# Layer 0's attention scores by column groups, with block transposes on VectorE and first sums as small products, in a two-layer attention kernel

## The chip, the cores and the metric

The kernel runs on one core of one Trainium2 chip. The core has five engines that work side by side, each with its own stream of instructions, which it runs in order, and which meet through semaphores: PE (TensorE, matrix products into PSUM), DVE (VectorE), ACT (ScalarE), POOL (GpSimd) and SP (which here only issues DMAs). The metric is device time in microseconds of one execution; lower is better.

## The reference, cut to what matters

The input `x` is 8 batches of 64 x 16 = 1024 tokens with 128 channels. Layer 0 is attention with 8 heads and a feed-forward part, with two softmaxes in a row over the keys, first over the 64 rows `m` and then over the 16 columns `g` of the 64 x 16 grid:

```python
q = proj(wq, bq); k = proj(wk, bk); v = proj(wv, bv)
scores = jnp.einsum('bhlfc,bhmgc->bhlfmg', q, k) / jnp.sqrt(jnp.float32(c))
a = jax.nn.softmax(scores, axis=4)
a = jax.nn.softmax(a, axis=5)
z = jnp.einsum('bhlfmg,bhmgc->bhlfc', a, v)
...
return _layer_norm(ffy + z1, ln2_g, ln2_b)
```

Layer 1 has an additive attention and a recurrence. For all pairs of the 1024 tokens of a batch it needs

```python
scores = jnp.einsum('d,bijd->bij', v, jnp.tanh(Wi[:, None, :, :] + Wi[:, :, None, :]))
```

and the recurrence `yt = sigmoid(wx_t + yt @ Vt)` runs over the tokens at the end.

## The kernel before

**An order written out by a planner.** `layer0` and `layer1` issue nothing themselves. They call `add`, which notes a piece of work: its engine (or a choice of engines) with an estimated cost, what it reads and writes, and a priority. `Plan.emit` (line 529) then simulates the engines with these costs and the latencies of lines 499 and 500 and writes every engine's instructions out in the order it finds. The order is fixed when the kernel is built; on the chip an engine that has to wait holds up all that stands behind it. `Bank` picks a free PSUM bank at that time, and `through_bank` (line 843) is the usual pair of a product into a bank and its eviction. For PE the planner knows two modes, "full" and "groups" (products of 32 array columns, four of which work side by side), and counts 0.1 us for a change.

**Layer 0** (line 872) goes over 8 heads and, in a head, 8 query tiles of 128 queries, 512 tiles over all batches. Keys and queries are folded into one matrix `A`, values and output into `Wvo`; `u` (line 903) is the projected query side and `vp` (line 917) the values. One tile does:

- scores (line 939, PE): two products of 512 columns into `sc`, 128 queries on the partitions and 1024 keys along them;
- the exponential (line 942, ACT), in place in PSUM;
- first sums over `m` (line 946, DVE), 1024 elements to 16, their inverse (949) and the division (952, DVE) from PSUM into `e` in SBUF. `sc` has two buffers and is free after that;
- for a pair of tiles: second exponential (963, ACT, 2048 elements), second sums over `g` (966, DVE), inverse (969), and the second division (980, POOL), in place;
- eight transposes of 128 x 128 (line 853, PE) a tile, four into a bank, each bank copied to `aT` (line 865, DVE, or 863, ACT, in batch 0), so that keys lie on partitions;
- attending (line 994, PE): for a pair of tiles eight products of 256 columns with `vp`, and their addition to `zs` (1001, DVE).

`e` has two buffers of a pair (`NE`), `aT` two. After the heads come a layer norm, the feed-forward part (lines 1041 to 1065, whose hidden values lie in an `aT`) and a second norm.

**Layer 1** (line 1218) takes the upper half of the token pairs in groups of rows. A row is `wiT` plus one column of it. Either ACT adds and takes the tanh at once (line 1107), or POOL or DVE (1117, 1111) add several rows into the ring `th` and ACT takes one wide tanh over them (line 1165). PE multiplies them with the vector `v` in column groups (line 1185) into `sa`. Which engine adds a row is the planner's choice, by which is free first and by the `fillers` of lines 1253 to 1261.

**Order.** Batch 0's layer 0 starts alone (`alone`), in two halves; it keeps the values of all eight heads in the ring `th`, and uses four banks in the first half. From then on layer 0 of batch b + 1 runs beside layer 1 of batch b. The last batch's layer 1 is alone again, and the recurrence (lines 1478 to 1520) ends the kernel.

Of the kernel before, what the change touches and what calls it, by code (L numbers as in the profile page):

```python
# [11 lines left out]
ALU = mybir.AluOpType  # L12
# [621 lines left out]
def fast_path(ctx: ExitStack, tc: tile.TileContext, a: dict, fits):  # L634
# [16 lines left out]
    NE = 2  # L651
# [11 lines left out]
    def ring(name, n, shape, pool=work):  # L663
        return [tile_of(pool, f"{name}{i}", shape) for i in range(n)]
# [20 lines left out]
    room = 20 * N  # L685
# [4 lines left out]
    aTs = ring("aT", 2, [P, NT, 2 * P])  # L690
    es = [wx[:, 4 + 2 * i : 6 + 2 * i, :] for i in range(NE)]
# [51 lines left out]


# [92 lines left out]
    count = {"aT": 0}  # L837

    def next_aT():
        count["aT"] += 1  # L840
        return (count["aT"] - 1) % 2

    def through_bank(pe, weight, r, evict, where, more, w, pri, choice=two):

        bank = Bank(*choice)
        n = len(plan.ops)
        add(("PE", weight), lambda _: pe(bank()), r=r, w=[("bank", n)], pri=pri, take=bank, wait=more + w)
        add(where, lambda e: evict(e, bank()), r=[("bank", n)] + more, w=w, pri=pri, give=bank)
# [23 lines left out]
    def layer0(b):  # L872
        alone = b == 0
        STRETCH = 0.95 if b < NB - 1 else 1.25
        xT, kx = xTs[b % 2], ("xT", b % 2)
        kz = ("zs",)
# [12 lines left out]
        for n_part, part in enumerate(parts):  # L889
# [3 lines left out]
            for h in range(H):  # L893
# [3 lines left out]
                if alone:  # L897
                    vp, kvp = th[:, (12 + h) * N : (13 + h) * N].rearrange("p (t c) -> p t c", c=C), ("vp0", h)
                for s in range(2) if part is None else (part,):
                    cols = slice(s * 512, (s + 1) * 512)  # L900

                    def project(bank, h=h, cols=cols):
                        nc.tensor.matmul(bank, A[:, h, :], xT[:, cols], start=True, stop=True)  # L903
# [20 lines left out]
                for qt in qts:  # L924
# [3 lines left out]
                    pair, q = (b * H * NT + i) // 2 % NE, qt % 2  # L928
# [3 lines left out]
                    r1, r2 = st[:, q, 0:G], st[:, :, G : G + M]  # L932
                    sc3 = sc.rearrange("p (m g) -> p m g", g=G)
                    e3 = e.rearrange("p (m g) -> p m g", g=G)

                    def scores(_, sc=sc, u=u, qt=qt):
                        for s in range(2):
                            cols = slice(s * 512, (s + 1) * 512)
                            nc.tensor.matmul(sc[:, cols], u[:, qt * P : (qt + 1) * P], xT[:, cols], start=True, stop=True)  # L939

                    add(("PE", 1.74), scores, r=[kx, ("u", h % 2, qt // 4)], w=[kc], pri=L0)
                    add(("ACT", 0.98), lambda _, sc=sc: nc.scalar.activation(sc, sc, AF.Exp, scale=SCALE),  # L942
                        r=[kc], w=[kc], pri=L0)

                    def first_sums(_, sc=sc, r1=r1):
                        nc.vector.tensor_reduce(r1, sc.rearrange("p (m g) -> p g m", g=G), AX.X, ALU.add)  # L946

                    def first_inverse(_, r1=r1):
                        nc.vector.reciprocal(r1, r1)

                    def divide(_, e3=e3, sc3=sc3, r1=r1):
                        nc.vector.tensor_tensor(e3, sc3, r1.unsqueeze(1).to_broadcast([P, M, G]), ALU.mult)  # L952

                    add(("DVE", 1.15), first_sums, r=[kc], w=[k1], pri=L0)
                    add(("DVE", 0.2), first_inverse, r=[k1], w=[k1], pri=L0)
                    add(("DVE", 1.22), divide, r=[kc, k1], w=[ke], pri=L0)
# [16 lines left out]
                    na = next_aT()  # L973
                    aT = aTs[na]
                    for q in range(2):
# [7 lines left out]
                        for s in range(2):  # L983
                            through_bank(
                                transposes([e[:, t * P : (t + 1) * P] for t in range(4 * s, 4 * s + 4)]), 0.52, [ke],
                                copy(aT[:, 4 * s : 4 * s + 4, q * P : (q + 1) * P]), evict(0.68), [],
                                [("aT", na, q, s)], L0, banks,
                            )
# [3 lines left out]
                    def attend(part, vp=vp, aT=aT, bank=bank):  # L992
                        for t in range(4 * part, 4 * part + 4):
                            nc.tensor.matmul(bank()[:, :256], vp[:, t, :], aT[:, t, :], start=t == 0, stop=t == NT - 1)  # L994

                    def gather(_, h=h, q0=q0, bank=bank):
                        zq = zs[:, q0 : q0 + 2 * P]
                        if h == 0:
                            nc.vector.scalar_tensor_tensor(zq, bank()[:, :256], zb, xT[:, q0 : q0 + 2 * P], ALU.add, ALU.add)
# [3 lines left out]
                    for s in range(2):  # L1003
                        add(
                            ("PE", 1.74), lambda _, attend=attend, s=s: attend(s),
                            r=[kvp + (p,) for p in range(2)] + [("aT", na, q, p) for q in range(2) for p in range(2)],
# [5 lines left out]
            for qh in range(2) if part is None else (part,):  # L1012
# [22 lines left out]
                na = next_aT()  # L1035
                hT = aTs[na].rearrange("p t q -> p (t q)").rearrange("p (f q) -> p f q", q=512)
                kh = [("aT", na, q, s) for q in range(2) for s in range(2)]
                for f in range(NFF):
# [10 lines left out]
                    through_bank(hidden, 0.9, [k1], relu, evict(0.75), kh[:1] if f else [], kh if f == 0 else [kh[f]], L0, banks)  # L1049
# [35 lines left out]
    def group(it, at0, r0, k, wiT, all_wi, L1, ROWS, fillers, chain, left, both, first_half):  # L1085
# [11 lines left out]
        slot = Span(ring_room, at[4], 12 * N if first_half else 20 * N)  # L1097
# [257 lines left out]
    def fetch_wx():  # L1355
        keys = [[("u", i, s) for s in range(2)] for i in range(2)]
        keys += [[("vp", i, s) for s in range(2)] for i in range(2)] + [[("e", i, q), ("e", i, 2)] for i in range(NE) for q in range(2)]
# [230 lines left out]
```

## Time and profile before

| | |
|---|---|
| median of 3 runs | 5320.47 us (5319.22 to 5320.98) |
| the profiled execution | 5316.93 us |
| its span, first to last instruction | 5315.0 us |
| granted clock of TensorE | 0.993 |
| share of the chain that ended last: scores, transposes, attending | 13%, 8%, 13% |
| share of the same chain: tanh times v | 25% |
| tanh on ACT: wide (997), single rows (1904) | 2734.8 us, 1369.8 us busy |

In the profile a group of instructions is given by its line, engine, operation, what it writes and reads, its shape and its count; then come the us in which it was busy, the mean ns of one, and the idle time of the engine before it with what ended that idle time. PE is the stream of products and PEld that of weight loads, which overlaps it. Ends of products are modelled, so PE's busy share is not its share at full speed.

### The profile page before, as it was taken

What the parts mean: (1) busy time and instruction counts of PE and PEld (TensorE: products, weight loads), DVE (VectorE), ACT (ScalarE), POOL (GpSimd) and SP (SyncE); (2) the same over time, 40 slices, a digit from 0 to 9 for tenths busy, and PEclk for the clock granted to TensorE, in tenths of its full rate; (3) what the DMA queues carried; (4) which work ended last, traced back from release to release, by engine and by line L of the source; (5) the groups of instructions that cost most, each with busy time, mean ns of one, the idle gap of its engine ahead of it and who ended that gap; (6) DMA issues with size and microseconds to landing.
All of it is one profiled execution on the core that took longest, in us unless ns stands there. A gap on an engine that the chain in (4) does not pass through costs nothing.

```text
span 5315.0 us, 98773 instructions
## 1 busy us (share of the span) xinstructions
PE 5007.1 (94%) x39173; PEld 2763.8 (52%) x39173; DVE 4884.6 (92%) x8676; ACT 5057.1 (95%) x4042; POOL 4522.8 (85%) x3113
## 2 busy tenths in 40 slices
PE   8899999999999999999999999999999999986567
PEld 6555555555555555555555455555555455542125
DVE  7899999999999999999999999999999999988885
ACT  5489999999999999999999999999999999999994
POOL 2365779899998999999998999999899999987991
PEclk9999999999999999999999999999999999999999
DMA  2000000000000000000000000000000000000001
GB/s 62 1 5 1 1 1 5 1 9 1 1 5 7 3 1 5 5 5 1 1 5 5 5 1 1 5 6 4 1 1 3 7 1 1 1 29 9 1 1 69
DMA packets 27335, 37.68 MB, mean 7 GB/s; under 512 B 2512, under 2 KB 19280, under 8 KB 26864
## 3 DMA queue, kind: packets, MB, share of 16 engines
q1 hardware_dynamic: 24832, 27.99, 1.6%
q8 instruction: 310, 5.08, 0.4%
q10 hardware_dynamic: 1872, 3.16, 0.2%
q14 instruction: 161, 1.32, 0.1%
q0 software_dynamic: 160, 0.13, 0.0%
HBM read 19.22 MB, written 12.06 MB: 6 GB/s over the span
## 4 chain that ended last, share of the span: by engine, by line
PE 67%; ACT 16%; DVE 10%; issue 6%; POOL 1%; DMA 0%; ACTq 0%; DVEq 0%; SPq 0%; POOLq 0%
PE sa L1185 25%; PE m L994 13%; PE sc L939 13%; ACT th L1165 9%; PE m L853 8%; ACT th L1107 4%; DVE th L1111 2%; PE m L1314 2%; PE m L917 2%; DVE stat_e L966 2%; PE m L903 1%; DVE stat_e L946 1%; ACT wx L963 1%; ACT sc L942 1%; DVE aT L865 1%
## 5 line engine op out<-in xcount | busy, mean ns | idle before, releaser
L1117 POOL TENSOR_TENSOR th<-wiT 128x1024 f32<-128x1024 f32 (+59 forms) x2303 | 3345.5, 1487 | 215.2 <-PE sa L1185 196.0
L1165 ACT ACTIVATE th<-th 128x2634 f32<-128x2634 f32 (+53 forms) x997 | 2734.8, 2774 | 9.3 <-DVE th L1117 6.0
L1185 PE MATMUL sa<-th,vpat 128*32 128x512 f32 (+36 forms) x24576 | 2009.0, 459 | 202.2 <-ACT th L1165 186.9
L1111 DVE TENSOR_SCALAR_CACHE_REDUCE th<-wiT 128x344 f32<-128x344 f32 (+59 forms) x1930 | 1602.9, 867 | 68.6 <-PE sa L1185 65.8
L1107 ACT ACTIVATE th<-wiT 128x512 f32<-128x512 f32 (+62 forms) x1904 | 1369.8, 793 | 11.8 <-PE sa L1185 11.8
L1185 PEld LDWEIGHTS sa<-th,vpat 128*32 128x32 f32 x24576 | 652.2, 110 | 1319.1 <-issue 842.2
L980 POOL TENSOR_TENSOR wx<-wx,stat_e 128x1024 f32<-128x1024 f32 x512 | 981.6, 1938 | 398.9 <-DVE stat_e L969 213.7
L939 PE MATMUL sc<-xT,wx 128*128 128x512 f32 x2048 | 983.5, 605 | 13.1 <-DVE wx L952 11.9
L994 PE MATMUL m<-aT,wx 128*128 128x256 f32 x3584 | 824.6, 384 | 7.2 <-DVE aT L865 7.2
L994 PEld LDWEIGHTS m<-aT,wx 128*128 128x128 f32 x3584 | 673.5, 191 | 187.8 <-issue 51.9
L865 DVE COPY aT<-m 128x512 f32<-128x512 f32 x940 | 616.6, 684 | 67.6 <-PE m L853 64.3
L946 DVE TENSOR_REDUCE stat_e<-sc 128x16 f32<-128x1024 f32 x512 | 613.5, 1204 | 38.9 <-ACT sc L942 37.7
L966 DVE TENSOR_REDUCE stat_e<-wx 128x128 f32<-128x2048 f32 x256 | 583.6, 2280 | 52.5 <-ACT wx L963 51.9
L952 DVE TENSOR_TENSOR wx<-sc,stat_e 128x1024 f32<-128x1024 f32 x512 | 619.9, 1214 | 3.2
L853 PEld LDWEIGHTS m<-ident,wx 128*128 128x128 f32 x3968 | 445.2, 141 | 309.4 <-issue 168.8
L942 ACT ACTIVATE sc<-sc 128x1024 f32<-128x1024 f32 x512 | 515.2, 1010 | 69.0 <-PE sc L939 52.8
L853 PE MATMUL m<-ident,wx 128*128 128x128 f32 x3968 | 558.6, 278 | 12.5 <-DVE aT L865 6.9
L939 PEld LDWEIGHTS sc<-xT,wx 128*128 128x128 f32 x2048 | 355.4, 191 | 385.8 <-issue 334.3
L963 ACT ACTIVATE wx<-wx 128x2048 f32<-128x2048 f32 x256 | 487.6, 1905 | 15.7 <-DVE wx L952 15.6
L969 DVE RECIPROCAL stat_e<-stat_e 128x128 f32<-128x128 f32 x256 | 240.9, 941 | 0.1
L1111 DVE DVE_READ_ACCUMULATOR th<-wiT 128x1 f32 x1930 | 160.8, 83 | 0.0
L917 PEld LDWEIGHTS m<-Wvo,xT 128*128 128x128 f32 x1080 | 133.9, 193 | 51.2 <-issue 25.0
(182 smaller groups left out, 2835.5 us busy)
## 6 DMA issues: line engine op xcount, KB each, us to landing
xT<-in_xt_dram SPq DMA_DIRECT2D x8, 512.0 KB, 3.6
th<-in_x_dram SPq DMA_DIRECT2D x8, 512.0 KB, 6.8
parked<-X SPq DMA_DIRECT2D x16, 256.0 KB, 2.3
xr<-parked SPq DMA_DIRECT2D x8, 512.0 KB, 8.1
parked_wx<-bT SPq DMA_DIRECT2D x14, 256.0 KB, 2.0
wx<-parked_wx SPq DMA_DIRECT2D x7, 512.0 KB, 3.2
out_dram<-ot ACTq DMA_DIRECT2D x8, 256.0 KB, 3.2
out_dram<-ot SPq DMA_DIRECT2D x8, 256.0 KB, 3.2
```

The costliest lines, as they stand in the source:

```text
L853: nc.tensor.transpose(bank[:, i * P : (i + 1) * P], s, ident)
L865: nc.vector.tensor_copy(dst, src)
L939: nc.tensor.matmul(sc[:, cols], u[:, qt * P : (qt + 1) * P], xT[:, cols], start=True, stop=True)
L946: nc.vector.tensor_reduce(r1, sc.rearrange("p (m g) -> p g m", g=G), AX.X, ALU.add)
L966: nc.vector.tensor_reduce(r2, e2.rearrange("p q (m g) -> p q m g", g=G), AX.X, ALU.add)
L980: nc.gpsimd.tensor_tensor(e3, e3, r2[:, q, :].unsqueeze(2).to_broadcast([P, M, G]), ALU.mult)
L994: nc.tensor.matmul(bank()[:, :256], vp[:, t, :], aT[:, t, :], start=t == 0, stop=t == NT - 1)
L1107: nc.scalar.activation(rows(c)[:, r, :], wiT[:, i0 + begin[c] :], AF.Tanh, bias=w_i(c, r))
L1111: nc.vector.tensor_scalar(rows(c)[:, r, :], wiT[:, i0 + begin[c] :], w_i(c, r), 0.0, ALU.add, ALU.add, accum_out=next_unused())
L1117: eng.tensor_tensor(rows(c), wiT[:, i0 + begin[c] :].unsqueeze(1).to_broadcast(shape), w_i(c).unsqueeze(2).to_broadcast(shape), ALU.add,)
L1165: nc.scalar.activation(slot()[:, a:z], slot()[:, a:z], AF.Tanh)
L1185: nc.tensor.matmul(sa[32 * c : 32 * c + 32, s:s1], vpat[:, 31 - r0 - r : 63 - r0 - r], rows(c)[:, r, s - at0 - begin[c] : s1 - at0 - begin ...
```

## The change

**Token order.** `xT` is now laid out by the host so that keys can be taken by quarters: token 256 a + 32 b + r stands at place 128 b + 32 a + r. `tokens` is a view of it by quarter `a`.

**Scores.** For each 32 queries (`s`) and each quarter of the keys (`a`) there is one product of 32 array columns and 256 keys, 16 a tile, in PE's "groups" mode. On partition 32 a + r lies query r of every block `s`, with the 256 keys of quarter `a`, for four values of `s` one after the other.

**First softmax.** The exponential goes from `sc` straight to `e`. Since a query's keys are now on four partitions, the first sums are products: 16 of 64 columns with `same_row` (a one where the partitions' numbers agree modulo 32) add over quarters and over four of the columns' parts, and a reduction of 64 elements on DVE finishes them. After the inverse, 16 products of 16 columns with slices of `ident` spread the result back to the four partitions, and DVE's division reads it from PSUM. The other branch (`by_pe` false) is not built.

**Transposes.** After the second division DVE transposes `e` in place in blocks of 32 x 32. With the keys' order this puts keys on partitions, so PE's transposes, their copies and `aT` are gone, and attending reads `e` itself, in runs of 32.

**Room.** `e` has three buffers, and the feed-forward part keeps its hidden values in one of them. The ring grows by 448 elements a partition; batch 0's values of heads 6 and 7 lie in `X1` and `B1`.

```diff
-    NE = 2
+    NE = 3
...
-    aTs = ring("aT", 2, [P, NT, 2 * P])
-    es = [wx[:, 4 + 2 * i : 6 + 2 * i, :] for i in range(NE)]
+    es = [wx[:, 4 + 2 * i : 6 + 2 * i, :] for i in range(2)] + ring("e", NE - 2, [P, 2, N])
...
+    same_row = tile_of(const, "same_row", [P, 32])
+    nc.vector.tensor_reduce(same_row, ident.rearrange("p (a r) -> p r a", a=4), AX.X, ALU.add)
...
+        tokens = xT.rearrange("p (b a r) -> p a b r", a=4, r=32)
...
                     def scores(_, sc=sc, u=u, qt=qt):
-                        for s in range(2):
-                            cols = slice(s * 512, (s + 1) * 512)
-                            nc.tensor.matmul(sc[:, cols], u[:, qt * P : (qt + 1) * P], xT[:, cols], start=True, stop=True)
+                        for s in range(4):
+                            rows = slice(qt * P + 32 * s, qt * P + 32 * s + 32)
+                            for a in range(4):
+                                nc.tensor.matmul(
+                                    sc[32 * a : 32 * a + 32, 256 * s : 256 * s + 256], u[:, rows],
+                                    tokens[:, a], start=True, stop=True,
+                                )
...
-                    add(("DVE", 1.15), first_sums, r=[kc], w=[k1], pri=L0)
-                    add(("DVE", 0.2), first_inverse, r=[k1], w=[k1], pri=L0)
-                    add(("DVE", 1.22), divide, r=[kc, k1], w=[ke], pri=L0)
...
+                        def sums(bank, e=e):
+                            for i in range(4):
+                                for s in range(4):
+                                    cols = slice(256 * s + 64 * i, 256 * s + 64 * i + 64)
+                                    nc.tensor.matmul(
+                                        bank[32 * s : 32 * s + 32, 0:64], same_row, e[:, cols], start=i == 0, stop=i == 3
+                                    )
...
+                        def last_sums(_, bank, s1=s1):
+                            nc.vector.tensor_reduce(
+                                s1, bank[:, 0:64].rearrange("p (m g) -> p g m", g=G), AX.X, ALU.add
+                            )
...
+                        through_bank(sums, 0.45, [ke], last_sums, ("DVE", 0.2), [], [k1], L0, banks, "groups")
...
+                        def spread(bank, r1=r1):
+                            for s in range(4):
+                                for a in range(4):
+                                    nc.tensor.matmul(
+                                        bank[32 * a : 32 * a + 32, s * G : s * G + G], ident[:, 32 * s : 32 * s + 32], r1,
+                                        start=True, stop=True,
+                                    )
...
+                        add(("DVE", 0.2), first_inverse, r=[k1], w=[k1], pri=L0)
+                        through_bank(spread, 0.3, [k1], divide, ("DVE", 1.22), [ke], [ke], L0, banks, "groups")
...
-                        for s in range(2):
-                            through_bank(
-                                transposes([e[:, t * P : (t + 1) * P] for t in range(4 * s, 4 * s + 4)]), 0.52, [ke],
-                                copy(aT[:, 4 * s : 4 * s + 4, q * P : (q + 1) * P]), evict(0.68), [],
-                                [("aT", na, q, s)], L0, banks,
-                            )
+                        add(("DVE", 1.17), lambda _, e=e: nc.vector.transpose(e, e), r=[ke], w=[ke], pri=L0)
...
+                    keys = e2.rearrange("p q (s b r) -> p b (q s) r", s=4, r=32)
...
-        "xt": np.asarray(x).reshape(NB, N, C).transpose(0, 2, 1),
+        "xt": np.asarray(x).reshape(NB, 4, 8, 32, C).transpose(0, 4, 2, 1, 3).reshape(NB, C, N),
```

## The prediction

> **What bounds the kernel now.** I read the page's busy shares and chain first, then busy time by stage, then the groups, then single stretches of TensorE's timeline.
>
> ```profile
> PE 5007.1 (94%) x39173; PEld 2763.8 (52%) x39173; DVE 4884.6 (92%) x8676; ACT 5057.1 (95%) x4042; POOL 4522.8 (85%) x3113
> ...
> PE 67%; ACT 16%; DVE 10%; issue 6%; POOL 1%; DMA 0%; ACTq 0%; DVEq 0%; SPq 0%; POOLq 0%
> ```
> ```profile
> 0.00:315.00 315.00, 282.19 (x1299) 197.81 (x1300) 259.80 (x359) 168.94 (x297) 113.07 (x76) 0.99 0.10 27
> 315.00:890.00 575.00, 565.42 (x3929) 324.01 (x3928) 539.51 (x806) 556.81 (x625) 419.72 (x263) 1.00 0.01 3
> 890.00:4490.00 3600.00, 3542.85 (x28053) 1936.49 (x28051) 3392.83 (x5937) 3573.75 (x2583) 3350.18 (x2306) 1.00 0.01 4
> ...
> 4800.00:5105.00 305.00, 181.03 (x2039) 59.28 (x2043) 259.77 (x531) 305.00 (x144) 253.37 (x166) 0.96 0.01 4
> ```
>
> A line of the second view gives, for a stretch, the busy us of PE, PEld, DVE, ACT, POOL, then the clock, the DMA share and GB/s. From 890 to 4490 us, six batches of about 600 us, ACT is busy 99%, PE 98%, DVE 94% and POOL 93%: nothing has room, and no one edit moves the end unless the others give way too. PE's ends are modelled, so 98% overstates it. From start to start its work for one batch is: 64 query tiles x 1.72 (scores) = 110; 64 x 0.87 (transposes) = 56; 32 x 3.45 (attending) = 110; 4.22 million tanh columns / 8 batches / 4 groups x 1.67 ns = 220, and 4 ns for each of 768 rounds, 3; projections, values, layer 1's products and FFN about 58; sum 557. The built order changes between full products and column groups 1730 times, 216 a batch at about 0.09 us: 19. So 576 of 600, 96%. ACT, whose durations are real, is the tighter bound; PE follows within 3%. In the first 315 us batch 0's layer 0 runs alone and DVE (218 of the 240 us from 60 to 300) leads; from 4800 ACT is never idle.
>
> ```profile
> L1165 ACT ACTIVATE th<-th 128x2634 f32<-128x2634 f32 (+53 forms) x997 | 2734.8, 2774 | 9.3 <-DVE th L1117 6.0
> ...
> L1107 ACT ACTIVATE th<-wiT 128x512 f32<-128x512 f32 (+62 forms) x1904 | 1369.8, 793 | 11.8 <-PE sa L1185 11.8
> ...
> L865 DVE COPY aT<-m 128x512 f32<-128x512 f32 x940 | 616.6, 684 | 67.6 <-PE m L853 64.3
> L946 DVE TENSOR_REDUCE stat_e<-sc 128x16 f32<-128x1024 f32 x512 | 613.5, 1204 | 38.9 <-ACT sc L942 37.7
> L966 DVE TENSOR_REDUCE stat_e<-wx 128x128 f32<-128x2048 f32 x256 | 583.6, 2280 | 52.5 <-ACT wx L963 51.9
> L952 DVE TENSOR_TENSOR wx<-sc,stat_e 128x1024 f32<-128x1024 f32 x512 | 619.9, 1214 | 3.2
> ```
> ```profile
> 276.95 1.88 PE L939 MATMUL sc<-xT,wx 128*128 128x512 f32 x4
> 278.67 1.04 PE L853 MATMUL m<-ident,wx 128*128 128x128 f32 x8
> 279.54 1.88 PE L939 MATMUL sc<-xT,wx 128*128 128x512 f32 x4
> ...
> 4361.02 1.09 PE L1185 MATMUL sa<-th,vpat 128*32 128x64 f32 x64
> 4362.04 1.98 PE L939 MATMUL sc<-xT,wx 128*128 128x512 f32 x4
> ```
>
> In the timeline the difference of two starts is what a piece costs: scores 1.72 us, eight transposes 0.87. The second stretch is the row nearest to the new small products: 64 records in column groups (each f32 product makes two), 61 to 64 columns wide, in 1.02 us with the change of mode behind them, four running side by side.
>
> **The change, part by part, for one query tile (512 in all).**
>
> *Scores.* Two products of 512 columns become 16 of 256 on 32 array columns, four at a time. L1185 shows that form: a round of four records takes its columns over 1.2 per ns and about 4 ns. Eight rounds of 256 columns: 8 x 0.218 = 1.74 us against 1.72. Equal. The operand is now read in runs of 32; no row here has that at this size. I take nothing; the far end is a tenth, 0.17 us.
>
> *Transposes go from PE (-0.87).* In their place PE gets sums, eight rounds of 64 columns, 8 x 0.058 = 0.46, and the spreading, eight rounds of 16 columns. Rows of 29 to 32 columns in L1185 run at about 32 ns a round, so 0.28 at most. **Here a rule speaks against the change**: the Trainium skill's TensorE: Matmul & The Clock Gate, in "Wait — 56ns, not 53.3ns?", says that starts never come closer than about 25 ns however narrow a product is. By it 64 records cost 1.6 us, not 0.74: 0.86 x 512 = 440 us more on PE, and the kernel becomes slower. The row above contradicts it for column groups (1.02 us over 64 records, 16 ns each, the change of mode included), in this kernel's own data type, so I take the row. PE: +0.02 - 0.87 + 0.46 + 0.28 = -0.11 us, a batch -7. In the built order mode changes fall from 1730 to 1206, 66 a batch less: -6. PE's batch becomes about 563.
>
> *First sums on DVE.* L946 is 1204 ns, of which 1024 elements at 0.96 per ns are 1067; the fixed 137 and 64 elements give 0.20. DVE -1.0 us. The inverse (236 ns) and the division (1214, one operand in PSUM as before) stay.
>
> *Copies (L865) become a block transpose.* Two copies, 2 x 0.684 = 1.37 us, against one 32x32 block transpose over 1024 elements. No row shows this operation. From below, a one-pass row: L1111's slope, 1.02 ns an element, 1.05 us. From above, two passes: L966 with 2048 elements, 2.28. The Trainium skill's Vector Engine (DVE) Microarchitecture Reference, section 3.8, says that the transposing front end sustains an element per cycle and lane; so I take the one-pass row with PSUM's fixed part, 1.21 (L952), and keep 2.28 as the far end. The skill's VectorE: DVE Perf Modes, "Rules for kernel authors", would leave a whole 128x128 transpose on TensorE; that rule counts neither the copy out of PSUM that TensorE's path needs (1.37) nor that PE is nearly full here.
>
> *DVE in sum*: -512 x 1.0 - 955 copies x 0.684 + 512 x 1.21 = -545 us. The planner hands this room to layer 1's rows. In the built orders DVE's single rows go from 1930 to 2362 (266 thousand more elements x 1.02 ns + 432 x 0.25 = +380), ACT's single tanh rows (L1107) from 1904 to 1544, wide tanh (L1165) from 997 to 1074, POOL's row additions from 2303 to 2254 (about -92 us by L1117). DVE ends near 4720, POOL near 4430.
>
> *ACT, the bound.* The tanh elements stay 4.22 million. A single row costs a fixed 0.2 us (L1107: 719 ns busy on a mean 600 elements, less 600 x 0.833), a wide pass 0.17: -360 x 0.22 + 77 x 0.17 = -66. First exponentials write SBUF: +5 at most (L942 1010 against L863's fixed part). 69 fewer copies in batch 0 save 41 us of ACT, but where ACT is busy only 54%: nothing for the end.
>
> *First stage.* From 60 to 300 us DVE serves 44 tiles. Per tile -1.204 - 0.58 (its 37 copies) + 0.20 + 1.21 = -0.37, 16 us in all, while PE changes mode oftener and three e buffers now hold a pair from the exponential until attending. I count 10.
>
> *Where stalls go.* `sc` comes free after the exponential instead of after the division: covered already (PE waited for L952 only 11.9 us). Behind a sums product that waits on ACT, or a spreading that waits on DVE's inverse, stand layer 1's tanh products, and behind those the row buffers, for which POOL already waited 196 us. I allow 10 us. Three e buffers at 19 us a pair give 56 us; the chain from exponential to attending is about 30 by the rows.
>
> *Sum*: 5315 - 66 + 5 - 10 + 10 = 5254. The profiled execution took 5316.9 in all (span plus 2), and the median, 5320.5, lies 3.5 above that: **5259 us**, 1.2% faster.
>
> **Rivals.** *A: the new meeting points stall PE (slower).* Each tile adds two places, 128 a batch, where in-order PE waits for a result ACT or DVE has just made, in place of the transposes' waits (13.1 us in the list of waits). PE's own 563 and today's 24 of slack-losses make 587; it overtakes a batch of 600 when each new place loses 0.10 us net. At 0.2 a batch is 613, seven and a half batches +97: 5415. For it: PE has no room. Against: the planner orders with latencies, and PE's visible waits before were small. *B: a slower block transpose (slower).* At two passes DVE gains 512 x 1.07 = 548 us, 68 a batch on about 545: 613, and with DVE busy 97% to 100% of a batch 5410 to 5550; it decides from about 1.8 us a transpose. Against: the one-pass reading. *C: more than forecast.* If batch 0 alone gains its 16 us, ACT's 45 us of idle between 315 and 4800 halves and the allowance is not needed: 5254 - 6 - 22 - 10 = 5216, median 5221. *D: it does nothing measurable*, stalls of about 0.09 us a place eating the gain: 5320.
>
> **Numbers.** Forecast 0.50, C 0.17, A 0.20, B (with the 25 ns floor) 0.07, D 0.06. What a measurement here can tell from no change is 0.2%, 10.6 us. Faster 0.67, same 0.07, slower 0.26. The likeliest case alone spans 5235 to 5290; with C below and A above, 5205 to 5415.
>
> **What would show it.** ACT still about 99% busy between 890 and 4490, with 1544 single rows; the block transpose near 1.2 us; the last sums near 0.2 us; 32 records of sums in 0.46 us and of spreading in 0.28 from start to start; DVE near 90% in the middle stage. It is wrong if PE shows waits of tens of us on the first exponential or on the inverse, if the transpose exceeds 1.8 us, if POOL's rows or second division (1938 ns) lengthen beside it, or if narrow records are 25 ns apart.

## The result and the profile after

The kernel after takes **5290.61 us** (median of 5 runs, 5288.59 to 5302.44) against 5320.47; the ratio is 0.9952 with a 95% interval of 0.9937 to 0.9966. It is faster by 30 us, 0.5%. The forecast was 61 us, so the sign is right and half of the gain is missing. The profiled execution of the kernel after took 5300.69 us (span 5298.8), one of the longer of its five, so that the two traces differ by 16 us and the medians by 30.

The page of the kernel after, first the busy times, then the chain that ended last, by engine:

```profile
PE 4915.6 (93%) x82181; PEld 3021.0 (57%) x82181; DVE 4739.3 (89%) x9090; ACT 4957.7 (94%) x3692; POOL 4437.4 (84%) x3064
...
PE 67%; ACT 15%; DVE 11%; issue 5%; POOL 1%; DMA 0%; SPq 0%; ACTq 0%; DVEq 0%; POOLq 0%
```

Every engine has less to do than before: PE by 92 us, DVE by 145, ACT by 99, POOL by 85. The forecast had DVE near 4720, POOL near 4430 and ACT 102 us lower; they came within 20 us. So the work left as planned, but the end moved by 30 us, about a third of what the least relieved engine lost (POOL, 85).

The groups of instructions of the kernel after that answer to the steps (counts, busy us, mean ns, idle time before and what ended it):

```profile
L1222 ACT ACTIVATE th<-th 128x3210 f32<-128x3210 f32 (+57 forms) x1074 | 2926.5, 2767 | 27.0 <-DVE th L1174 15.6
L1242 PE MATMUL sa<-th,vpat 128*32 128x512 f32 (+33 forms) x24576 | 2045.9, 460 | 243.4 <-ACT th L1222 222.9
...
L1164 ACT ACTIVATE th<-wiT 128x501 f32<-128x501 f32 (+59 forms) x1544 | 1120.2, 797 | 16.1 <-PE sa L1242 14.9
...
L990 DVE TENSOR_TENSOR wx<-wx,m 128x1024 f32<-128x1024 f32 x330 | 396.9, 1206 | 38.6 <-PE m L982 36.8
L956 ACT ACTIVATE wx<-sc 128x1024 f32<-128x1024 f32 x342 | 340.3, 1022 | 93.8 <-PE sa L1050 35.9
L1042 DVE STREAM_TRANSPOSE wx<-wx 128x1024 f32<-128x1024 f32 x342 | 417.6, 1230 | 4.1 <-POOL wx L1039 3.6
```

The block transpose costs 1.23 us (1.21 was taken), the division 1.21, the first exponential 1.02. TensorE's waits for the wide tanh rose from 187 to 223 us over the whole kernel; the division waits 58 us for the spreading, 37 of them in the group shown.

In the timeline of TensorE (start, us, work, idle time before it) the two small products stand like this:

```profile
4360.23 0.44 PE L982 MATMUL m<-stat_e,ident 128*32 128x16 f32 x32 [2.06 <-DVE stat_e L977]
4360.50 1.55 PE L1242 MATMUL sa<-th,vpat 128*32 128x416 f32 x16
4364.29 0.65 PE L965 MATMUL m<-wx,same_row 128*32 128x64 f32 x32 [2.24 <-DVE zs L1058]
4364.76 3.18 PE L1242 MATMUL sa<-th,vpat 128*32 128x32 f32 x80
```

From start to start the spreading takes 0.27 us and the sums 0.47; 0.28 and 0.46 had been forecast.

**Where the time went.** To compare equal amounts of layer 1's work I cut both traces at two instructions that both have: the ninth and the 39th of the 46 exponentials of layer 1's own softmax on ACT (line 1281 before, 1338 after). They start at 1194.8 and 4806.6 us before, and at 1198.8 and 4787.4 after. Busy time by engine in these stretches (length, then PE, PEld, DVE, ACT, POOL), of the kernel before:

```profile
0.00:1194.80 1194.80, 1151.58 (x7560) 689.91 (x7561) 1084.31 (x1672) 1030.08 (x1144) 809.49 (x535) 1.00 0.03 10
1194.80:4806.60 3611.80, 3533.74 (x28178) 1926.23 (x28177) 3400.73 (x6091) 3585.57 (x2609) 3360.66 (x2325) 1.00 0.02 5
```

and of the kernel after:

```profile
0.00:1198.80 1198.80, 1139.51 (x20522) 751.65 (x20523) 1001.04 (x1673) 978.40 (x999) 791.68 (x520) 0.99 0.04 11
1198.80:4787.40 3588.60, 3449.44 (x58217) 2121.71 (x58217) 3326.26 (x6492) 3534.30 (x2395) 3293.70 (x2290) 0.99 0.02 5
```

The first stretch became 4 us longer, although ACT lost 52 us of work there and DVE 83; PE, busy 96% of it before, lost 12. The middle became 23 us shorter, while PE lost 84, DVE 74, ACT 51 and POOL 67: ACT's idle time went from 26 to 54 us. The rest, from the later mark to the end, is 508 us before and 511 after. So half of ACT's saving fell in a stretch that did not become shorter, and half of what remained was turned into idle time. The three parts add up to the 16 us by which the two traces differ; where the other 14 us of the medians' 30 lie, the traces cannot say.

**The granted clock.** TensorE's mean granted clock fell from 0.993 before to 0.987 after. It falls in slices of 3.4 us, or a few of these in a row, in which the clock stands at 0.50. In the kernel before one of them runs from 152.0 to 155.4 us (first a line as above, with the clock as third figure from the end, then TensorE's timeline):

```profile
152.00:155.40 3.40, 3.40 (x8) 1.74 (x7) 1.08 (x1) 1.84 (x2) 0.00 (x0) 0.50 0.01 2
```
```profile
151.50 3.27 PE L939 MATMUL sc<-xT,wx 128*128 128x512 f32 x4 [0.59 <-DVE wx L952]
154.55 1.02 PE L853 MATMUL m<-ident,wx 128*128 128x128 f32 x4
155.41 0.61 PE L853 MATMUL sa<-ident,wx 128*128 128x128 f32 x4
155.85 1.88 PE L939 MATMUL sc<-xT,wx 128*128 128x512 f32 x4
157.57 0.60 PE L994 MATMUL sa<-aT,th 128*128 128x256 f32 x2
```

The scores that start 0.5 us before it take 3.05 us from start to start, those behind it 1.72. Up to the later mark PE is busy for 20 us in such slices before and for 74 us after. If products take twice as long there, PE's busy time holds 10 us of this before and 37 after: at an equal clock PE would have been spared some 22 us in the first stretch, not 12, and some 100 in the middle, not 84. This is an estimate; no run holds the clock, so what it costs the end was not shown.

### The profile page after: what moved, and what is told of

It is laid out like the page before. It is cut to its first block, busy times and chain, and to the rows that moved or that the text cites. A ratio compares the mean times of both kernels' runs of the same rounds, so it can differ in the third digit from the quotient of the medians.

```text
span 5298.8 us, 184474 instructions
## 1 busy us (share of the span) xinstructions
PE 4915.6 (93%) x82181; PEld 3021.0 (57%) x82181; DVE 4739.3 (89%) x9090; ACT 4957.7 (94%) x3692; POOL 4437.4 (84%) x3064
## 3 DMA queue, kind: packets, MB, share of 16 engines
q8 instruction: 645, 10.57, 0.9%
## 4 chain that ended last, share of the span: by engine, by line
PE 67%; ACT 15%; DVE 11%; issue 5%; POOL 1%; DMA 0%; SPq 0%; ACTq 0%; DVEq 0%; POOLq 0%
PE sa L1242 23%; PE sc L948 14%; PE m L1050 13%; ACT th L1222 10%; DVE th L1168 3%; PE m L965 3%; ACT th L1164 3%; PE m L923 2%; PE m L982 2%; PE m L1371 2%; DVE stat_e L1027 2%; PE m L909 1%; DVE wx L990 1%; DVE th L1174 1%; PE m L1120 1%
## 5 line engine op out<-in xcount | busy, mean ns | idle before, releaser
L1174 POOL TENSOR_TENSOR th<-wiT 128x1024 f32<-128x1024 f32 (+55 forms) x2254 | 3255.7, 1479 | 308.9 <-PE sa L1242 270.3
L1222 ACT ACTIVATE th<-th 128x3210 f32<-128x3210 f32 (+57 forms) x1074 | 2926.5, 2767 | 27.0 <-DVE th L1174 15.6
L1242 PE MATMUL sa<-th,vpat 128*32 128x512 f32 (+33 forms) x24576 | 2045.9, 460 | 243.4 <-ACT th L1222 222.9
L1168 DVE TENSOR_SCALAR_CACHE_REDUCE th<-wiT 128x344 f32<-128x344 f32 (+61 forms) x2362 | 1945.8, 863 | 79.6 <-PE sa L1242 76.3
L1164 ACT ACTIVATE th<-wiT 128x501 f32<-128x501 f32 (+59 forms) x1544 | 1120.2, 797 | 16.1 <-PE sa L1242 14.9
L948 PE MATMUL sc<-xT,wx 128*32 128x256 f32 x16384 | 980.3, 380 | 2.2 <-issue 2.2
L948 PEld LDWEIGHTS sc<-xT,wx 128*32 128x32 f32 x16384 | 549.9, 110 | 291.4 <-issue 45.5
L1050 PE MATMUL m<-wx 128*128 128x256 f32 x2400 | 563.1, 388 | 18.6 <-DVE stat_e L970 7.7
L1050 PEld LDWEIGHTS m<-wx 128*128 128x128 f32 x2400 | 449.6, 192 | 146.2 <-issue 45.6
L956 ACT ACTIVATE wx<-sc 128x1024 f32<-128x1024 f32 x342 | 340.3, 1022 | 93.8 <-PE sa L1050 35.9
L1042 DVE STREAM_TRANSPOSE wx<-wx 128x1024 f32<-128x1024 f32 x342 | 417.6, 1230 | 4.1 <-POOL wx L1039 3.6
```

What stands on the lines that cost most here:

```text
L948: nc.tensor.matmul(sc[32 * a : 32 * a + 32, 256 * s : 256 * s + 256], u[:, rows], tokens[:, a], start=True, stop=True,)
L1042: add(("DVE", 1.17), lambda _, e=e: nc.vector.transpose(e, e), r=[ke], w=[ke], pri=L0)
L1050: nc.tensor.matmul(bank()[:, :256], vp[:, t, :], keys[:, t], start=t == 0, stop=t == NT - 1)
L1164: nc.scalar.activation(rows(c)[:, r, :], wiT[:, i0 + begin[c] :], AF.Tanh, bias=w_i(c, r))
L1168: nc.vector.tensor_scalar(rows(c)[:, r, :], wiT[:, i0 + begin[c] :], w_i(c, r), 0.0, ALU.add, ALU.add, accum_out=next_unused())
L1174: eng.tensor_tensor(rows(c), wiT[:, i0 + begin[c] :].unsqueeze(1).to_broadcast(shape), w_i(c).unsqueeze(2).to_broadcast(shape), ALU.add,)
```

## The experiments

Times are medians; the kernel before took 5318 to 5321 us beside each of them. "After" below is the 5291 us of the kernel after.

### Are three buffers for `e` too few in the first stage?

In the kernel after, `e` is held until attending, and in the first 315 us ACT waits 69 us for attending to give it back (36 of them in the group at L956 above). First a control with a smaller ring `th`, then a fourth buffer in the room this frees for all batches, then a fourth buffer for batch 0 alone.

```diff
-    room = 20*N+448
+    room = 18*N+192
```

> The changed kernel with layer 1's ring of rows cut by 2304 elements a partition (18 N + 192 in place of 20 N + 448), three buffers of e as before: the control for the next run. Both theories: a smaller ring can only make rows wait, 0 to 20 us slower than the changed kernel's 5291, so 5290 to 5310.

Measured: 5319.98 us (5316.92 to 5335.41), ratio 1.001 (1.000 to 1.002), 29 us above after.

```diff
-    NE = 3
+    NE = 4
...
-    room = 20*N+448
+    room = 18*N+192
```

> The same cut ring, and the freed room as a fourth buffer of e. Theory E (the exponential now writes e, so a buffer is held from the exponential to attending, about 31 us in the first stage, and three are too few): 49 tiles by 312 us become 54 or more, and ScalarE's waits for attending (69 us in the first 315 us, 25 us after) shrink to under 20 us; 30 to 45 us below the control. Theory M (the two new meeting points of TensorE with ScalarE and VectorE per tile eat the gain): within 10 us of the control.

Measured: 5365.37 us, ratio 1.0084 (1.0067 to 1.0100), 45 us slower than its control. By 312 us it had done 52 first exponentials, the control 48: the fourth buffer does speed up the first stage of layer 0, and still the end comes later.

```diff
+    es.append(th[:, 18 * N : 20 * N].rearrange("p (q n) -> p q n", n=N))
...
-                    pair = pair if q else next_e()
+                    pair = pair if q else next_e(NE + 1 if alone else NE)
...
-    room = 20*N+448
+    room = 20*N+192
```

> The changed kernel with a fourth buffer of e for batch 0's layer 0 only, in the upper end of the ring, which layer 1 does not use by then; the ring keeps its size but for 256 elements. Theory E: the first stage gains 20 to 35 us, 5255 to 5270 in all, with what stays lost after 315 us unchanged. Theory M: 5285 to 5295.

Measured: 5318.02 us, ratio 1.0001 (0.9992 to 1.0011), 27 us slower than after, with 53 first exponentials by 312 us (after 48) and the first of layer 1's softmax exponentials at 451 us (after 393). The wait for a buffer was real; with it gone, layer 0 runs ahead and layer 1 starts later. So a fourth buffer does not bring the missing gain back, as my theory had it. But each of these kernels is also another planned order, and an order alone can move the time by as much (below): that the wait costs nothing is not shown.

### What are the small products worth?

The branch that isn't built in the kernel after does the first sums on DVE, as before, and only their total over four partitions on PE:

```diff
-                    by_pe = True
+                    by_pe = False
```

> The changed kernel with the first sums back on VectorE (1024 elements to 64), one small product of four for the totals, the inverse of 64 elements, and the division from the scores in PSUM: column groups and block transposes stay. A buffer of e is held from the division only, and TensorE meets the others once less per tile. Theory M: the waits at sums and spreading go, TensorE's load falls by about 0.6 us a tile, but VectorE gets 1.3 us more a tile; if the waits were the larger part, 5290 or less. Theory E: the first stage recovers (54 tiles by 312 us), but VectorE is the bound there and later: 5320 to 5380.

Measured: 5371.05 us, ratio 1.0098 (1.0081 to 1.0115), 80 us slower than after. DVE's work rose by 202 us to 4941.6, PE's fell by 160, ACT's rose by 60. PE with less to do did not help, and its granted clock fell to 0.974. So in this order the first sums are better on PE. The size of the 80 us is uncertain, since orders of the same work differ by up to 69 us (below).

### Which engine is the bound of the kernel before?

Each of the next kernels keeps the planned order and cuts about 200 us (by the rows' durations) from one engine, in layer 0; the fifth makes all four cuts.

```diff
# PE: attending over 6 of 8 key tiles
-                        for t in range(4 * part, 4 * part + 4):
+                        for t in ((0, 1), (4, 5, 6, 7))[part]:
# ACT: the second exponential over half of the keys of each tile
-nc.scalar.activation(e2, e2, AF.Exp)
+nc.scalar.activation(e2[:, :, 0:512], e2[:, :, 0:512], AF.Exp)
# DVE: first sums over 640 of 1024 keys
-nc.vector.tensor_reduce(r1, sc.rearrange(
+nc.vector.tensor_reduce(r1, sc[:, 0:640].rearrange(
# POOL: second division over 768 of 1024 keys
-                            e3 = e.rearrange("p (m g) -> p m g", g=G)
+                            e3 = e[:, 0:768].rearrange("p (m g) -> p m g", g=G)
...
```

> The kernel before with TensorE's work cut and everything else, the order of all instructions too, left as it is: attending takes six of its eight key tiles (key tiles 2 and 3 are left out of the result), 0.86 us less per pair, 219 us in all. Theory ACT (ScalarE's busy time sets the end, as the prediction had it): 0 to 60 us less than 5320. Theory PE (TensorE's place in a fixed order sets it): 120 us less or more.

> The kernel before with ScalarE's work cut by about the same amount in the same order: the second exponential runs over half of its 2048 elements (the other half keeps the first softmax's values), 0.85 us less per pair, 218 us in all. Theory ACT: 120 to 190 us less than 5320, until TensorE's load holds it. Theory PE: less than 60 us.

> The kernel before, in its own order of work, with the 512 first sums of layer 0 reduced over 640 of the 1024 keys (the sums are then of fewer keys; nothing else changes): about 0.45 us less for each, some 205 to 230 us less work on VectorE, as much as was taken off ScalarE and off TensorE alone before. Theory ScalarE is the bound (the forecast's): VectorE has idle time of 435 us, so nothing comes back, 5315 to 5320. Theory coupled engines (in a fixed order each engine in turn is the one waited for): a part comes back, as for the other two, 20 to 60 us, 5260 to 5300.

> The kernel before, in its own order, with GpSimd's division of the second softmax made over 768 of the 1024 keys (the last quarter stays undivided): about 0.41 us less for each of the tiles that it divides, some 200 us less work on GpSimd, whose 4523 us of work are the fewest of the four. Theory ScalarE is the bound: no gain, 5315 to 5320. Theory coupled engines: GpSimd is one link of every pair's chain, so the latency of the chain falls too, 10 to 40 us back, 5280 to 5310.

> The kernel before with the four cuts of these runs at once: attending over 6 of 8 key tiles, the second exponential over half of the keys of each of its tiles, the first sums over 640 of 1024 keys, the second softmax's division over 768 of 1024. Each engine then has 200 to 220 us less to do. Theory coupled engines: the cuts that returned 28 us (TensorE) and 28 us (ScalarE) alone return far more together than the sum of the four single returns, 150 to 210 us, 5110 to 5170. Theory of a separate delay (a fixed chain of latencies or the transfers set the end): the returns only add up, 60 to 120 us, 5200 to 5260.

| the kernel before with less work on | us | ratio, 95% interval | returned (us, from the medians) |
|---|---|---|---|
| PE | 5290.12 | 0.9945, 0.9929 to 0.9962 | 28 |
| ACT | 5290.25 | 0.9946, 0.9929 to 0.9963 | 28 |
| DVE | 5307.29 | 0.9978, 0.9969 to 0.9988 | 11 |
| POOL | 5306.25 | 0.9974, 0.9965 to 0.9984 | 12 |
| all four | 5100.77 | 0.9591, 0.9575 to 0.9607 | 217 |

With a single cut the page's busy time fell by 149 us on PE, 196 on ACT, 180 on DVE and 220 on POOL. ACT's 28 us are far below the 120 to 190 of the theory that ACT is the bound, and DVE's 11 us lie between the two ranges stated for it. The four single returns add up to 79 us; together the cuts return 217, all of what each engine was spared (the busy times on the page fell by 212 on PE, 215 on DVE, 217 on ACT, 223 on POOL). This is the plainest answer of the study: **ACT is not the bound; nor is any one engine.** How it looks in the middle stage is shown by its busy times, in the kernel with less on PE,

```profile
890.00:4490.00 3600.00, 3448.44 (x27491) 1809.98 (x27482) 3399.07 (x5960) 3585.94 (x2594) 3365.31 (x2317) 1.00 0.01 4
```

with less on ACT,

```profile
890.00:4490.00 3600.00, 3558.05 (x28208) 1944.58 (x28210) 3405.64 (x5964) 3453.04 (x2595) 3369.40 (x2318) 1.00 0.01 4
```

and with less on all four:

```profile
890.00:4490.00 3600.00, 3541.89 (x28674) 1881.39 (x28673) 3388.78 (x6213) 3576.44 (x2716) 3344.44 (x2426) 1.00 0.01 4
```

Relieve PE, and it is busy 95.8% while ACT goes to 99.6%; relieve ACT, and it is busy 95.9% while PE goes to 98.8%. Relieve all, and every figure but PEld is again within 0.2% of that of the kernel before: the whole is scaled down. In each single case most of the spared time becomes idle time of the relieved engine, whose next piece of work waits for another engine in an order that was written out beforehand.

### And of the kernel after?

The same cuts of PE, ACT and POOL; on DVE here the block transposes over 640 of 1024 columns:

```diff
-nc.vector.transpose(e, e)
+nc.vector.transpose(e[:, 0:640], e[:, 0:640])
```

> The changed kernel with the same cut on TensorE (six of eight key tiles in attending, 219 us), same order. Theory ACT: 0 to 60 us less than 5291. Theory M (TensorE late at the new meeting points makes ScalarE idle): 80 us less or more, and ScalarE's idle time falls from 341 us to about 260.

> The changed kernel with the same cut on ScalarE (second exponential over half, 218 us), same order. Theory ACT: 120 to 190 us less than 5291. Theory M: less than 80 us.

> The kernel after, in its own order, with the block transposes on VectorE made over 640 of 1024 columns (the other keys' weights stay untransposed): 0.46 us less for each of 512, some 230 us less work on VectorE. If the block transposes on VectorE hold up the pairs in the new order (each pair needs two of them between GpSimd's division and the attending), 50 us or more come back, 5230 to 5250. If the engines are merely coupled, 15 to 40 us, 5250 to 5280. If VectorE has time to spare, none, 5285 to 5295.

> The kernel after, in its own order, with four cuts at once: attending over 6 of 8 key tiles, the second exponential over half of the keys of each of its tiles, the block transposes over 640 of 1024 columns, the second softmax's division over 768 of 1024 keys: 200 to 230 us less work on each engine. Theory coupled engines: as in the kernel before (218 us), the return is about that of the least-cut engine, 190 to 225 us, 5065 to 5100. If the new order has slack of its own on top of the engines' work (a delay that isn't work), less comes back, 100 to 170 us, 5120 to 5190.

| the kernel after with less work on | us | ratio to before, 95% interval | returned (us, against 5290.61) |
|---|---|---|---|
| PE | 5235.89 | 0.9846, 0.9829 to 0.9862 | 55 |
| ACT | 5267.73 | 0.9910, 0.9893 to 0.9926 | 23 |
| DVE | 5295.36 | 0.9955, 0.9938 to 0.9971 | none (5 longer) |
| all four, with POOL | 5059.61 | 0.9518, 0.9498 to 0.9538 | 231 |

All four together again return all (busy times fell by 229 on PE, 230 on DVE, 217 on ACT, 218 on POOL). I had counted with 190 to 225, so even a little more came than the least-cut engine was spared. Alone, PE now returns twice what it did before, and DVE (by another cut than before) nothing: the balance has moved from DVE towards PE. Where the returns arise is seen between the same two exponentials as above. With less on PE,

```profile
0.00:1164.70 1164.70, 1086.88 (x20233) 696.78 (x20234) 997.16 (x1675) 976.20 (x998) 793.24 (x520) 0.98 0.04 11
1164.70:4725.50 3560.80, 3341.04 (x57488) 1982.70 (x57487) 3322.03 (x6495) 3528.00 (x2394) 3291.25 (x2289) 0.99 0.02 5
```

and with less on ACT:

```profile
0.00:1193.60 1193.60, 1135.64 (x20516) 751.67 (x20517) 997.17 (x1672) 917.07 (x999) 790.32 (x519) 0.99 0.04 11
1193.60:4748.70 3555.10, 3437.28 (x58224) 2120.33 (x58223) 3319.52 (x6495) 3402.80 (x2395) 3295.16 (x2291) 0.99 0.02 6
```

In the first stretch the cut on PE returns 34 us of 53, that on ACT 5 of 61: there PE is the one that the others wait for. In the middle the two are alike, 28 us of 108 and 34 of 132.

### Do the new meeting points stall PE?

Rival A of the prediction. Both small products take a constant row in place of the exponential and of the inverse; same records, same places, but no wait for ACT's or DVE's result (the first softmax is divided by a constant's sum). Their waits for a free bank remain.

```diff
-                                        bank[32 * s : 32 * s + 32, 0:64], same_row, e[:, cols], start=i == 0, stop=i == 3
+                                        bank[32 * s : 32 * s + 32, 0:64], same_row, g2_sb[:, 0:64], start=i == 0, stop=i == 3
...
-                                        bank[32 * a : 32 * a + 32, s * G : s * G + G], ident[:, 32 * s : 32 * s + 32], r1,
+                                        bank[32 * a : 32 * a + 32, s * G : s * G + G], ident[:, 32 * s : 32 * s + 32], g2_sb[:, 0:G],
```

> The kernel after, in the same planned order, where the two new small products of every query tile take a constant row (64 and 16 columns of a row of the second layer norm's weights) in place of the exponential and of the inverse: the same records of the same shapes are issued in the same places, but TensorE waits at neither of them, and the first softmax is divided by a constant's sum (so the output differs). Rival A (the meeting points stall TensorE): 30 to 60 us come back, about 5235 to 5260. Theory order (the price of the new work is as forecast and the rest of the gain is lost in how the planner's order meets the real durations everywhere): at most 10 us, 5280 to 5295.

Measured: 5302.01 us (5295.85 to 5305.47), ratio 0.9968 (0.9955 to 0.9980): not shorter than after but 11 us longer, just outside both ranges. TensorE's list of waits from 1195 to 4790 us, of the kernel after,

```profile
PE sa L1242 <- ACT th L1222: 65.3, 77, 3.4
PE m L1050 <- DVE stat_e L970: 9.9, 9, 2.5
PE m L1050 <- DVE e L1042: 9.8, 2, 7.2
```

and of this kernel in the same stretch

```profile
PE sa L1242 <- ACT th L1222: 67.7, 76, 3.4
PE m L1050 <- DVE stat_e L970: 10.2, 9, 2.5
PE m L1050 <- DVE e L1042: 8.5, 2, 7.2
```

(us in total, times, the longest) are the same within 3 us: TensorE waits for the tanh, not at the new products. In the kernel before the same list begins with

```profile
PE sa L1185 <- ACT th L1165: 31.1, 39, 2.1
```

Rival A is refuted for the data waits. The waits of the two products for a free bank were not tried apart; in the list of the kernel after they show as 4.1 and 3.1 us.

### How much is the order itself worth?

The same work in other orders. The planner's price of the first exponential is set near what the traces show (1.01 us before, 1.02 after), in both kernels; then, in the kernel after, its head start for layer 0 and its price of the block transpose.

```diff
-add(("ACT", 0.98), lambda _, sc=sc
+add(("ACT", 1.02), lambda _, sc=sc
```

> The kernel after, with nothing changed but the planner's price of the first exponential, 1.02 in place of 0.98 us as both traces show it: the same work in another order. Theory order (an order's luck is worth some 30 us either way): anything in 5255 to 5325, differing from 5291 by 10 us or more. Theory of a fixed new cost (the waits at the small products take what is missing, whatever the order): within 8 us of 5291.

> The kernel before with the same new price of the first exponential in the plan, 1.02 in place of 0.98 us: the same work in another order. Theory order: it differs from 5320 by 10 us or more, 5285 to 5355. Theory of a fixed new cost: within 8 us of 5320.

```diff
-    LEAD, DOWN, SOON, LATE = 0.35, 0.06, 0.5, -0.3
+    LEAD, DOWN, SOON, LATE = 0.30, 0.06, 0.5, -0.3
```

> The kernel after with the planner's head start of layer 0 over layer 1 (LEAD) at 0.30 in place of 0.35 of a batch: the same work in another order. Theory order: it differs from 5291 by 10 us or more, 5255 to 5325. Theory of a fixed new cost: within 8 us of 5291.

```diff
-add(("DVE", 1.17), lambda _, e=e: nc.vector.transpose(e, e)
+add(("DVE", 1.23), lambda _, e=e: nc.vector.transpose(e, e)
```

> The kernel after, with nothing changed but the planner's price of the block transpose, 1.23 us in place of 1.17 as the trace shows it: the same work in another order. Theory order: anything in 5255 to 5360, differing from 5291 by 10 us or more. Theory of a fixed new cost: within 8 us of 5291. A time under 5280 would be a version that beats both kernels.

| | us | ratio to before, 95% interval |
|---|---|---|
| after, exponential priced 1.02 | 5356.17 | 1.0067, 1.0050 to 1.0084 |
| before, exponential priced 1.02 | 5381.64 | 1.0118, 1.0101 to 1.0135 |
| after, LEAD 0.30 | 5297.02 | 0.9952, 0.9937 to 0.9967 |
| after, transpose priced 1.23 | 5287.00 | 0.9944, 0.9925 to 0.9963 |

The first two missed even the wide span that I gave them: 0.04 us in a price of the plan costs 61 us in the kernel before and 66 in the kernel after. The other two stayed within 8 us of after, so that not every new order moves the time. The four orders of the kernel after that have the same ring and buffers lie between 5287 and 5356 us, the three kernels with changed rings or buffers between 5318 and 5365. A new order can thus cost more than the change gives; none of those tried gave a clear gain. Yet the change itself comes out alike in both pairs: 30 us with the plan's old price and 25 us with the new one (5381.64 less 5356.17). The last kernel is within the spread of after, so no version here clearly beats it.

By stage the second pair differs from the first. Between the same two exponentials of layer 1's softmax, with the new price, the kernel before has

```profile
0.00:1208.40 1208.40, 1161.46 (x7578) 694.39 (x7579) 1094.66 (x1679) 1019.50 (x1078) 823.93 (x544) 0.99 0.03 10
1208.40:4878.70 3670.30, 3545.53 (x28161) 1927.56 (x28159) 3439.84 (x6198) 3576.09 (x2554) 3385.92 (x2341) 0.99 0.02 5
```

and the kernel after

```profile
0.00:1223.20 1223.20, 1148.21 (x20641) 757.89 (x20645) 1015.76 (x1711) 979.41 (x988) 788.22 (x519) 0.98 0.04 11
1223.20:4842.70 3619.50, 3450.39 (x58111) 2120.13 (x58104) 3364.06 (x6455) 3528.48 (x2367) 3329.84 (x2304) 0.99 0.02 5
```

Here the first stretch became 15 us longer and the middle 51 us shorter, while ACT was spared 48 us in the middle: the whole of it came back, and ACT's idle time there stayed (94 and 91 us).

## Where the prediction held, and where it failed

**Unit costs: right.** Scores, sums, spreading, transpose, division, single rows (1544) and wide passes (1074) came as forecast, and with them the busy time of DVE, ACT and POOL; from 890 to 4490 us ACT is busy 98% and DVE 92%. Between the floor of 25 ns that the Trainium skill states (TensorE: Matmul & The Clock Gate, "Wait — 56ns, not 53.3ns?") and the row with 16 ns a record, taking the row was right: 32 records of sums took 0.47 us, 32 of spreading 0.27, which is 15 and 8 ns each. For these products in column groups that floor does not hold.

**"ACT, the bound", -66: the step that failed.** The prediction saw that "nothing has room, and no one edit moves the end unless the others give way too", and then took ACT as "the tighter bound; PE follows within 3%" and put ACT's saving into the sum at its full value. ACT's saving in the middle was 51 us between the marks, near the forecast; the stretch became 23 us shorter, and 28 us turned into ACT's idle time. That a saving on ACT does not count in full by itself is shown by the single cuts: some 200 us less on ACT returned 28 us in the kernel before and 23 in the kernel after, and the same on PE 28 and 55. A busy share of 99% beside one of 98% does not make an engine the bound.

These single prices do not explain the 30 us either. At 28, 28, 11 and 12 us for about 200 each, the savings of 92, 99, 145 and 85 us on PE, ACT, DVE and POOL would be worth 13 + 14 + 8 + 5 = 40 us; but savings that come together returned in full with all four cuts, and in the middle all four engines were spared at least 51 us here. With the plan's other price the middle did return ACT's saving in full (51 us for 48). So whether it comes back depends on the order: the prediction took one number, with 10 us for stalls, where a changed price in the plan made a difference of some 30.

**"First stage": -10 forecast, +4 measured** (up to the earlier mark, which lies later than the 315 us of the forecast). DVE was taken to lead there, and its relief came (83 us by the mark). But PE was as full: from 60 to 300 us it is busy for 217 us where DVE is for 218, and from 0 to 315, in the prediction's own line, for 282 against 260. It was relieved by 12 us only, and by the estimate above the lower clock, for which the prediction has no term, took some 10 us of its relief. The single cuts in the kernel after show PE as the one that leads (34 us returned of 53). In the pair with the other price the first stretch became longer too, by 15 us, with PE relieved by 13. So this step failed in both orders.

**Stalls, +10.** By the marks, 14 us of the difference from forecast lie in the first stage. In the middle, ACT's idle time rose by 28 us. That the data waits of the new meeting points cause it is refuted (without them ACT is idle for 53 us there, with them for 54); three buffers are not shown to cause it, since a fourth did not lower it. ACT's list of waits from 1195 to 4790 us (us in total, times, the longest) shows where they stand. In the kernel before it begins with

```profile
ACT sc L942 <- PE sc L939: 9.0, 19, 1.2
ACT th L1165 <- DVE th L1117: 6.0, 2, 3.8
ACT wx L963 <- DVE wx L952: 3.0, 3, 2.3
```

and in the kernel after with

```profile
ACT th L1222 <- DVE th L1174: 13.4, 3, 7.2
ACT wx L956 <- PE m L1050: 11.4, 11, 2.4
ACT wx L956 <- PE sc L948: 9.7, 18, 1.0
```

Two are new or longer: three wide tanh that wait for their rows, and 11.4 us in which the first exponential waits for attending to give back `e`. The second looks like a cause, but the kernel with four buffers for all batches tells against it, as far as one other order can. Its list over the same work (the same two exponentials as marks, 1245 to 4855 us) begins

```profile
ACT e L956 <- PE sc L948: 16.7, 28, 3.0
ACT th L1222 <- DVE th L1168: 14.9, 4, 9.6
ACT th L1222 <- POOL th L1174: 11.2, 7, 3.5
```

The wait for attending is no longer among the longest, and ACT is idle for 72 us (3610.5 less 3538.9 busy), where its control with three buffers is idle for 59:

```profile
1244.60:4855.10 3610.50, 3450.32 (x57890) 2111.59 (x57877) 3322.06 (x6469) 3538.88 (x2394) 3295.87 (x2286) 0.99 0.02 6
```
```profile
1212.20:4807.30 3595.10, 3449.63 (x58151) 2117.09 (x58144) 3288.56 (x6462) 3536.23 (x2410) 3259.34 (x2267) 0.99 0.02 5
```

A wait taken away comes back at another place. Between the same marks ACT's idle time is 26 and 94 us in the two orders of the kernel before, and 36 to 91 in the four of the kernel after with the same ring and buffers. So 28 us are within what an order makes; which feature of this order costs them was not shown, nor how much of them the lower clock does (some 16 us of PE's time in the middle, by the estimate above), and both stay open.

**The rivals.** A and B did not come: over the whole kernel PE waits 5.8 us for the inverse and 3.2 us for the first exponential at the new products, and a transpose takes 1.23 us. C had batch 0 gain its 16 us, which did not happen. D, no measurable gain, did not come either: 30 us are well above 10.6. The measured time lies just above the likeliest case's own span (5235 to 5290), between it and D. That it came so near to D is not for D's reason, stalls at the new places: without their data waits the kernel was no shorter.

## What to carry to other kernels

Where several engines are above 90% busy in a fixed order, a saving on one of them is worth a fraction of itself: here between nothing and a quarter of the planned cut alone, and all of it when all engines gave way together in an unchanged order. Before a sum takes an engine as the bound, take 4% of its work away in the present order and see what comes back; if a like cut of its neighbour returns as much, none is the bound. Stage by stage, ask which engine is not relieved: in the first stage here it was PE, and the stage returned nothing. And compare a change, stage by stage, in more than one order of the same work, since one order is one draw.

## What the runs showed of the hardware that was not expected

- Products of 16 columns in column groups are no closer than the prediction's rows of 29 to 32 columns: 32 records in 0.27 us from start to start, 8 ns a record.
- Though PE was busy for 93% of the span, its granted clock fell to half in slices of 3.4 us. PE was mostly busy in them (115 of 143 us in the kernel after), and the scores in one of them took 3.05 us instead of 1.72.
- The change nearly doubles the instructions, from 98773 to 184474, and the bytes of instructions fetched, from 5.08 to 10.57 MB. No cost of it was seen: time put down to issue in the chain that ended last went from 6% to 5%.
